# Filter layers in bfloat16 over stacked parts, and old rows of x fetched early, in a graph layer on one Trainium2 core

## The chip, the cores and the metric

The kernel runs on one core of a Trainium2 chip. Its engines are named as in the profile: PE (TensorE, the matrix products; its weight loads are PEld), DVE (VectorE), ACT (ScalarE), POOL (GpSimd) and SP (SyncE, which here only issues DMAs). Each takes its instructions in order and waits for the others by semaphores. The metric is the device time of one execution in microseconds (us).

## The reference

A graph layer with continuous filters: 12,500 nodes with 128 features (`x`), 400,000 edges sorted by target `dst` (used as the gathering index), each with 20 edge features and a weight. `smu` is a smooth activation made of a linear term and one with erf.

```python
h    = relu(layernorm(x))                       # 12500 x 128
h    = h @ W_in2f.T
Wij  = smu(edge_attr_20 @ W_f1.T + b_f1) @ W_f2.T + b_f2
Wij  = Wij * edge_weight[:, None]               # 400000 x 128
x_ij = h[dst] * Wij
agg  = segment_sum(x_ij, src, 12500)
out  = x + smu(agg @ W_o1.T + b_o1) @ W_o2.T + b_o2
```

Writing `z = f @ W_f1.T + b_f1`, the kernel uses smu(z) = gelu-like(z) + LIN * z up to a factor that is put into `w_f2`: the activation has a bent part and a linear part.

## The kernel before

Edges are cut into 3125 tiles of 128, four tiles make a group (512 edges, 782 groups), two groups a supertile (1024 edges, 391 supertiles). The supertiles are divided into nine stages ("epochs") of 59, 59, 59, 59, 48, 37, 27, 27 and 16 supertiles. Nodes are cut into 98 blocks of 128 (`NB`).

In stage k each group's messages are computed and scattered, row by row, into the DRAM buffer `buf{k}`, where each of the 98 blocks of source nodes has a fixed number of slots. While stage k runs, the buffer of stage k-1 is read back (`rw`) and summed into `agg` with products against selection matrices `se` (L690, L703, L716). After the last group comes a tail, in which the buffer of the last stage is summed and the output layers run.

The order of PE, DVE, ACT and SP is written out by hand; POOL's follows from the program. One pass of the main loop, for group g, holds steps of several groups:

- SP: `load(s + 3)` on every second group: the 20 feature rows of a supertile into one of four `fbufs` (L438), the targets broadcast over 128 partitions, `rbc` (L448), and two windows of `h`, `hw` (L462). Besides, SP clears the next stage's buffer (L178) and fetches `rw` of the stage before (L679), each waiting for the PE product that frees its buffer.
- `hide(g + 2)`: PE product of `w_f1` (row 20 of it is the bias, against a row of ones; the rows behind are zero) with the features, float32, 512 columns, into `pu` (L562). `bend(g + 2)`: ACT's gelu from `pu` to `ge` (L570). `smooth(g + 2)`: DVE adds LIN * `pu` to `ge`, giving `sm` (L578).
- `count`, `bins`, `read`, `number`: slots of the scattered rows, on DVE (L496, L540, L549) and PE (L510 to L513).
- `pick`: DVE one-hot of the targets (L471); `gather(g + 1)`: PE picks the rows of `h` (L596); `take`: ACT copies them (L604).
- `weigh(g + 1)`: PE product of `w_f2` with `sm`, float32, 512 columns, into `pw` (L615). `mix(g + 1)`: DVE multiplies (L625).
- `turn(g)`: four PE products of the messages with `w_o1` (L635). `send(g)`: ACT scales them by the edge weight `w_sb` into one of six `ms` buffers (L642, L645), and POOL issues four indirect DMAs of 128 rows each (L648), with the slot numbers `ix`.
- `parts`: PE and DVE work for the sums of the stage before.

During the first stage, `step()` deals out a list of small preparations among the groups: the rows of `h` in three bfloat16 parts each (L204 to L227, tiles `hs`), the targets, late weights, `output_bias` at the end. `hs` tiles come from the `edge` pool, two buffers.

In the tail (from L944), `ask()` fetches a unit (four blocks) of old rows of x on ACT's queue (L243) into an `hg` or `mt` tile and has POOL add the bias (L249); four units are asked for ahead, then one after each `store()`. `between()` adds agg and its gelu on POOL (L981) into an `sm` tile, `second_half()` multiplies by `w_o2` on PE (L263), `store()` adds the old rows on DVE (L267) and sends the unit out on SP (L269).

`w_sb` (edge weights), `hi_f` and `lo_b` (numbers of the source's block and row) each have a column a tile for all 3125 tiles and are read in order of the groups.

## Time and profile before

| | us |
|---|---|
| median of 3 runs | 4114.15 |
| the runs | 4108.7, 4114.17, 4114.15 |
| the profiled execution | 4108.47 |
| its span, first to last instruction | 4106.6 |
| first scatter starts | 19.9 |
| last scatter starts | 4001.5 |

The profiler's page gives the busy time of each engine, groups of instructions by line with their mean duration, and the idle time of the engine just before them with what ended most of it. "Issue" there is time in which the engine waited for nothing that the profile shows. A timeline lists instructions with start and duration. DMA share is the busy share of the 16 DMA engines. Queue q1 carries the DMAs that SP issues, q0 those of POOL. The costliest groups besides those shown below:

```profile
L645 ACT ACTIVATE ms<-pt,w_sb 128x128 f32<-128x128 f32 x3125 | 889.0, 368 | 1122.7 <-PE pt L635 1115.4
L703 PE MATMUL pg<-se,rw 128*128 128x128 f32 x8036 | 1149.1, 280 | 2.9 <-DVE se L690 2.9
L615 PE MATMUL pw<-sm,w_f 128*128 128x512 f32 x1564 | 823.0, 609 | 10.7 <-DVE sm L578 8.8
L562 PE MATMUL pu<-f,w_f 128*128 128x512 f32 x1564 | 807.3, 598 | 0.0
L578 DVE SCALAR_TENSOR_TENSOR sm<-pu,ge 128x512 f32<-128x512 f32 x782 | 535.8, 685 | 185.6 <-ACT ge L570 179.2
L596 PE MATMUL ph<-oh,hw 126*128 126x512 bf16 x770 | 297.0, 386 | 0.0
...
q1 hardware_dynamic: 449760, 601.83, 54.7%
q0 software_dynamic: 100320, 207.40, 15.9%
```

A float32 product appears as two matmul records; the busy time is that of their union.

### The profile page before, as it was taken

The page shows a single profiled execution, that of the slowest core. Times are in us where ns is not written, and L with a number is a line of the kernel's source. Part 1 is how long each engine was busy: PE and PEld are TensorE (multiplying, and loading weights), DVE is VectorE, ACT ScalarE, POOL GpSimd, SP SyncE. Part 2 cuts the span into 40 slices and gives each one's busy share as a digit, 9 for nine tenths or more (in the row PEclk, how much of TensorE's full clock was granted, in tenths as well). Part 3 has the DMA queues.
Part 4 walks back from the last instruction along what each step waited for, and adds up shares of the span by engine and source line. Part 5 has one row for each costly group of instructions (what it writes and reads, how often), then busy time and mean ns, then how long its engine had stood idle before and what let it go on. Part 6 is the DMA issues. An engine that isn't in the chain of part 4 may idle for free.

```text
span 4106.6 us, 74086 instructions
## 1 busy us (share of the span) xinstructions
PE 3668.0 (89%) x21117; PEld 2553.0 (62%) x21117; DVE 3445.1 (84%) x7657; ACT 1948.2 (47%) x5690; POOL 3081.7 (75%) x3199
## 2 busy tenths in 40 slices
PE   7878887998979998979998979999899989999897
PEld 4445545666656666646666656666677667666677
DVE  8898887888868888868888868888899889988896
ACT  4557764544444444434544434444444444444441
POOL 6777777777777777777777777777777777777775
PEclk9999999999999999999999989999999999999999
DMA  6976656776647676757667747777689699887568
GB/s 188 232 189 179 195 166 198 204 201 197 195 130 220 204 204 186 201 152 206 202 197 198 198 147 204 208 204 212 179 229 223 186 244 242 221 228 217 164 194 250
DMA packets 564246, 820.83 MB, mean 200 GB/s; under 512 B 178033, under 2 KB 378488, under 8 KB 563698
## 3 DMA queue, kind: packets, MB, share of 16 engines
q1 hardware_dynamic: 449760, 601.83, 54.7%
q0 software_dynamic: 100320, 207.40, 15.9%
q10 hardware_dynamic: 13746, 6.80, 0.6%
q8 instruction: 167, 2.74, 0.3%
q14 instruction: 253, 2.07, 0.2%
HBM read 442.34 MB, written 373.37 MB: 199 GB/s over the span
## 4 chain that ended last, share of the span: by engine, by line
PE 38%; DVE 28%; DMA 19%; ACT 6%; issue 5%; POOL 2%; DVEq 0%; SPq 0%; ACTq 0%; POOLq 0%
DMA buf<-ms,ix 17%; PE pt L635 11%; PE pg L703 8%; DVE se L690 8%; PE pw L615 8%; PE pu L562 7%; DVE mt L625 5%; DVE so L496 4%; DVE sm L578 3%; DVE sl L540 3%; ACT ms L645 2%; ACT ge L570 2%; POOL buf L648 2%; PE ph L596 2%; DVE agg L716 1%
## 5 line engine op out<-in xcount | busy, mean ns | idle before, releaser
L648 POOL DMA_INDIRECT buf<-ms,ix x3125 | 3011.3, 964 | 981.5 <-issue 384.1
L645 ACT ACTIVATE ms<-pt,w_sb 128x128 f32<-128x128 f32 x3125 | 889.0, 368 | 1122.7 <-PE pt L635 1115.4
L635 PE MATMUL pt<-w_o,mt 128*128 128x128 f32 x6250 | 883.7, 285 | 386.0 <-DVE mt L625 382.4
L703 PEld LDWEIGHTS pg<-se,rw 128*128 128x128 f32 x8036 | 1052.5, 192 | 246.5 <-issue 209.7
L703 PE MATMUL pg<-se,rw 128*128 128x128 f32 x8036 | 1149.1, 280 | 2.9 <-DVE se L690 2.9
L635 PEld LDWEIGHTS pt<-w_o,mt 128*128 128x128 f32 x6250 | 768.5, 194 | 472.9 <-DVE mt L625 468.9
L496 DVE SCALAR_TENSOR_TENSOR so<-irow_ps,hi_f,so 128x98 f16<-128x98 f32 x3116 | 989.5, 318 | 82.6
L615 PE MATMUL pw<-sm,w_f 128*128 128x512 f32 x1564 | 823.0, 609 | 10.7 <-DVE sm L578 8.8
L562 PE MATMUL pu<-f,w_f 128*128 128x512 f32 x1564 | 807.3, 598 | 0.0
L625 DVE SCALAR_TENSOR_TENSOR mt<-pw,b,hg 128x512 f32<-128x512 f32 x782 | 583.9, 747 | 201.3 <-ACT hg L604 198.0
L570 ACT ACTIVATE ge<-pu 128x512 f32<-128x512 f32 x782 | 468.4, 599 | 533.2 <-PE pu L562 524.6
L578 DVE SCALAR_TENSOR_TENSOR sm<-pu,ge 128x512 f32<-128x512 f32 x782 | 535.8, 685 | 185.6 <-ACT ge L570 179.2
L690 DVE TENSOR_TENSOR se<-irow_ps,rw 128x1536 f32<-128x1536 f32 (+1 forms) x345 | 588.0, 1704 | 114.0 <-DMA rw<-buf 109.1
L604 ACT ACTIVATE hg<-ph 128x512 f32<-128x512 f32 x782 | 468.5, 599 | 59.7 <-PE ph L596 42.9
L540 DVE TENSOR_REDUCE sl<-pc 128x4 f32<-128x392 f32 x782 | 434.7, 556 | 0.0
L642 ACT ACTIVATE ms<-lo_b 128x4 f32<-128x4 bf16 x782 | 160.1, 205 | 339.8 <-DMA buf<-ms,ix 339.4
L596 PE MATMUL ph<-oh,hw 126*128 126x512 bf16 x770 | 297.0, 386 | 0.0
L562 PEld LDWEIGHTS pu<-f,w_f 128*128 128x128 f32 x1564 | 251.9, 195 | 52.2 <-issue 40.9
L510 PE MATMUL pc<-so,tri 128*128 128x392 f16 x782 | 257.8, 330 | 0.4 <-DVE so L496 0.2
L615 PEld LDWEIGHTS pw<-sm,w_f 128*128 128x128 f32 x1564 | 241.3, 195 | 23.6 <-DVE sm L578 20.2
L512 PEld LDWEIGHTS <-rest_h 128*128 128x128 f16 x781 | 76.3, 98 | 263.1 <-issue 263.1
L512 PE MATMUL pc<-so,rest_h 128*128 128x294 f16 x781 | 225.5, 289 | 0.0
(153 smaller groups left out, 1386.9 us busy)
## 6 DMA issues: line engine op xcount, KB each, us to landing
rw<-buf SPq DMA_DIRECT2D x292, 774.0 KB
rbc<-rel_dram SPq DMA_DIRECT2D x389, 256.0 KB
buf<-zero SPq DMA_DIRECT2D x243, 387.0 KB
buf<-ms,ix POOLq DMA_INDIRECT x3125
buf<-zero SPq DMA_DIRECT2D x193, 258.0 KB
rw<-buf SPq DMA_DIRECT2D x49, 645.0 KB
f<-in_f_t SPq DMA_DIRECT2D x390, 80.0 KB
hw<-h_dram SPq DMA_DIRECT2D x770, 31.5 KB
```

The lines of the kernel that those rows point to most:

```text
L496: nc.vector.scalar_tensor_tensor(so[:, j], irow_ps[:, :NB], hi_f[:, t + j:t + j + 1], so[:, j - 1] if j else before, op0=ALU.is_equal, op1 ...
L540: nc.vector.tensor_reduce(sl[:, :n], pc[:, :n], op=ALU.max, axis=AX.X)
L562: nc.tensor.matmul(pu[:, :n], w_f1, loaded[g // PER][0][:, o:o + n], start=True, stop=True)
L570: nc.scalar.activation(ge[:, :n], units_of[g][:, :n], AF.Gelu, scale=ZS)
L578: nc.vector.scalar_tensor_tensor(sm[:, :n], units_of.pop(g)[:, :n], LIN, hidden[g][:, :n], op0=ALU.mult, op1=ALU.add)
L615: nc.tensor.matmul(pw[:, :n], w_f2, hidden.pop(g)[:, :n], start=True, stop=True)
L625: nc.vector.scalar_tensor_tensor(mt[:, :n], pws.pop(g)[:, :n], b2, rows_of.pop(g)[:, :n], op0=ALU.add, op1=ALU.mult)
L635: nc.tensor.matmul(pt[:, j, :], mt[:, j * P:(j + 1) * P], w_o1, start=True, stop=True)
L645: nc.scalar.activation(ms[:, j, 0:P], pt[:, j], AF.Copy, scale=w_sb[:, t + j:t + j + 1])
L648: i = nc.gpsimd.indirect_dma_start(out=bufs[k][:, :], out_offset=bass.IndirectOffsetOnAxis(ap=ix[:, j:j + 1], axis=0), in_=ms[:, j, :], in ...
L690: nc.vector.tensor_tensor(se[:, :m], irow_ps.unsqueeze(1).to_broadcast([P, m, P]), rows_in[c][:, :m, P:P + 1].to_broadcast([P, m, P]), op= ...
L703: nc.tensor.matmul(pgs[0][:, g, :], rows_in[c][:, o, 0:P], sel[c][:, o, :], start=(q == 0), stop=(q == Q[k] - 1))
```

## The change

From supertile 60 on (`PLAIN`; the 61st) the two filter products use bfloat16 parts. Each float32 number is written as a sum of three bfloat16 parts, and of the nine products of parts the six largest are kept. Twenty features times six products are 120 rows, and three more rows hold the parts of the bias against ones: 123 of 128 rows, one bfloat16 pass. `ws_f` holds the stacked weights of `w_f1`. `ws_c` holds those of LIN * `w_f1` * `w_f2`, the linear term of smu carried through the second layer; it is accumulated in `pw` ahead of `w_f2` times the gelu. So `smooth` does nothing for these groups.

The features come in chunks of six supertiles (`SEG`): one DMA brings 120 rows to `fx`, ACT and DVE cut them into three parts (`split`, in two halves of 512 columns each: eight steps over eight groups, two of each kind), and three DMAs a supertile copy the parts inside SBUF into the stacked rows, 60, 40 and 20 of them. Three `fbufs` of float32 remain and serve as six bfloat16 stacks; their last 32 rows are filled with bfloat16 ones. `rbc` has three buffers in place of four, `hs` tiles grow.

Six steps at the end of the list of preparations make the weights. In the last stage, one unit of old rows a group, twelve in all, is fetched on SP's queue into columns of `w_sb`, `hi_f` and `lo_b` that have been read for the last time; in the tail `ask()` fetches only the others. The tail's `sm` moves to the `msg` pool.

```diff
-    b1w = const.tile([P, P], F32, name="b1w")
...
-    lo_b = const.tile([P, NT], BF, name="lo_b")
+    lo_w = const.tile([P, NT + NT % 2], BF, name="lo_b")
+    lo_b = lo_w[:, 0:NT]
...
+    ws_f = const.tile([P, P], BF, name="ws_f")
+    ws_c = const.tile([P, P], BF, name="ws_c")
...
-        NF = 4
+        NF = 3
+        HALVES = 2
+        SEG = P // R
+        PLAIN = eps_of[0][1] + 1
         fbufs = [ld.tile([P, SUP * P], F32, name=f"f{i}", bufs=1) for i in range(NF)]
+        fx = ld.tile([P, SUP * P], F32, name="fx", bufs=1)
         def fill(i, engine):
             engine.memset(fbufs[i], 1.0)
+            engine.memset(fbufs[i][96:P, :].bitcast(BF), 1.0)
+        def stack_of(s):
+            half = s // NF % HALVES
+            return fbufs[s % NF].bitcast(BF)[:, half * SUP * P:(half + 1) * SUP * P]
...
-        fill(3, nc.gpsimd)
...
-            if s > 0:
+            if s >= PLAIN:
+                fb = stack_of(s)
+                c, j = (s - PLAIN) // SEG, (s - PLAIN) % SEG
+                a = 0
+                for q in range(3):
+                    r = 3 - q
+                    nc.sync.dma_start(fb[a:a + r * R, :n],
+                                      parts_of[c][j * R:(j + 1) * R, q, :n].unsqueeze(1).to_broadcast([R, r, n]))
+                    a += r * R
+            elif s > 0:
                 nc.sync.dma_start(fb[0:R, :n], f_t[:, e0:e0 + n])
...
+        def split(c, i):
...
+                    nc.sync.dma_start(fx[0:whole * R, :],
+                                      f_t[:, e0:e0 + whole * SUP * P].rearrange("k (s e) -> s k e", e=SUP * P))
...
+            f32, of = fx[:rows, o:o + w], lambda q: part[:rows, q, o:o + w]
+            if kind == 0:
+                nc.scalar.activation(of(0), f32, AF.Copy)
+            elif kind == 1:
+                nc.vector.tensor_sub(f32, f32, of(0))
+            elif kind == 2:
+                nc.scalar.activation(of(1), f32, AF.Copy)
+            else:
+                nc.vector.tensor_sub(of(2), f32, of(1))
+        def splits(g):
+            c, i = divmod(g - PER * (PLAIN - 3 - SEG) - 4, PER * SEG)
+            if c >= 0 and i < 8:
+                split(c, i)
+            if c >= -1 and i == 8:
+                split(c + 1, -1)
...
-            rb = ld.tile([P, SUP * P], BF, name="rbc")
+            rb = ld.tile([P, SUP * P], BF, name="rbc", bufs=3)
...
-            nc.tensor.matmul(pu[:, :n], w_f1, loaded[g // PER][0][:, o:o + n], start=True, stop=True)
+            w = w_f1 if g // PER < PLAIN else ws_f
+            nc.tensor.matmul(pu[:, :n], w, loaded[g // PER][0][:, o:o + n], start=True, stop=True)
...
-            sm = edge.tile([P, GRP * P], F32, name="sm")
-            nc.vector.scalar_tensor_tensor(sm[:, :n], units_of.pop(g)[:, :n], LIN, hidden[g][:, :n],
-                                           op0=ALU.mult, op1=ALU.add)
-            hidden[g] = sm
+            pu, ge = units_of.pop(g), hidden[g]
+            if g // PER < PLAIN:
+                nc.vector.scalar_tensor_tensor(ge[:, :n], pu[:, :n], LIN, ge[:, :n], op0=ALU.mult, op1=ALU.add)
...
-            nc.tensor.matmul(pw[:, :n], w_f2, hidden.pop(g)[:, :n], start=True, stop=True)
+            folded = g // PER >= PLAIN
+            if folded:
+                nc.tensor.matmul(pw[:, :n], ws_c, loaded[g // PER][0][:, o:o + n], start=True, stop=False)
+            nc.tensor.matmul(pw[:, :n], w_f2, hidden.pop(g)[:, :n], start=not folded, stop=True)
...
+        def homes():
+            spent = eps_of[-1][0] * SUP // (GRP * P) * (GRP * P)
+            for t in (w_sb, hi_f):
+                for o in range(0, spent, GRP * P):
+                    yield t[:, o:o + GRP * P]
+            for o in range(0, spent // 2 // (GRP * P) * (GRP * P), GRP * P):
+                yield lo_w.bitcast(F32)[:, o:o + GRP * P]
+        held = {unit: home.rearrange("p (b d) -> p b d", b=GRP)
+                for unit, home in zip([u for u in units if u[1] == GRP][::2], homes())}
+        ahead = list(held)
...
+        def crossed():
+            nc.gpsimd.memset(ws_f, 0.0)
+            nc.gpsimd.memset(ws_c, 0.0)
...
+        def stacked():
+            for w, to in zip((ws_f, ws_c), pieces()):
+                a = 0
+                for q in range(3):
+                    r = 3 - q
+                    nc.sync.dma_start(w[a:a + r * R, :], to[0:R, 0:r, :])
+                    a += r * R
+                for q in range(3):
+                    nc.sync.dma_start(w[a + q:a + q + 1, :], to[R:R + 1, q, :])
...
+        weight_steps = [crossed, combined, lambda: cut_weights(w_f1, pieces()[0]), lambda: cut_weights(lift, pieces()[1]),
+                        stacked, restored]
...
+        steps += weight_steps
...
+            if k and k == EPOCHS - 1 and i >= WAIT and ahead:
+                unit = ahead.pop(0)
+                old_rows(unit, held[unit], nc.sync)
...
             smooth(g + 2)
+            splits(g)
...
-                xr = edge.tile([P, GRP * P], F32, name=name).rearrange("p (b d) -> p b d", b=GRP)
-                old_rows(unit, xr, nc.scalar)
+                if unit in held:
+                    xr = held[unit]
+                else:
+                    xr = edge.tile([P, GRP * P], F32, name=name).rearrange("p (b d) -> p b d", b=GRP)
+                    old_rows(unit, xr, nc.scalar)
...
-            sm = edge.tile([P, GRP * P], F32, name="sm")
+            sm = msg.tile([P, GRP, ROW], F32, name="ms").rearrange("p b r -> p (b r)")[:, :GRP * P]
```

More of the change, by code (lines that the diff above doesn't have):

```diff
@@ L284, in gnn_kernel @@
         nc.vector.tensor_copy(irow_ps, irow)
-        NF = 4
+        NF = 3
+        HALVES = 2
+        SEG = P // R
+        assert SEG >= 6 and 6 * R + 3 <= P
+        PLAIN = eps_of[0][1] + 1
         fbufs = [ld.tile([P, SUP * P], F32, name=f"f{i}", bufs=1) for i in range(NF)]
+        fx = ld.tile([P, SUP * P], F32, name="fx", bufs=1)
         def fill(i, engine):
             engine.memset(fbufs[i], 1.0)
+            engine.memset(fbufs[i][96:P, :].bitcast(BF), 1.0)
+        def stack_of(s):
+            half = s // NF % HALVES
+            return fbufs[s % NF].bitcast(BF)[:, half * SUP * P:(half + 1) * SUP * P]
         FEW = 6 * SUP
         def parts_tile():
-            return edge.tile([P, GRP, 3, D], BF, name="hs")
+            whole = edge.tile([P, 3, SUP * P], BF, name="hs").rearrange("p q e -> p (q e)")
+            return whole[:, :GRP * 3 * D].rearrange("p (n k d) -> p n k d", k=3, d=D)
         early = (eps_of[0][1] + 3) * PER
@@ L441, in load, with chunk_of @@
                 targets(s)
+        parts_of = {}
+        def chunk_of(c):
+            s0 = PLAIN + c * SEG
+            return s0, min(SEG, NS - s0)
+        def split(c, i):
+            s0, m = chunk_of(c)
+            if m <= 0:
+                return
+            e0, whole = sups[s0][0] * P, sum(sups[s0 + j][1] == SUP for j in range(m))
+            rows = m * R
+            cols = sups[s0][1] * P if m == 1 else SUP * P
+            if i < 0:
+                if whole:
+                    nc.sync.dma_start(fx[0:whole * R, :],
+                                      f_t[:, e0:e0 + whole * SUP * P].rearrange("k (s e) -> s k e", e=SUP * P))
+                for j in range(whole, m):
+                    n = sups[s0 + j][1] * P
+                    e = sups[s0 + j][0] * P
+                    nc.sync.dma_start(fx[j * R:(j + 1) * R, :n], f_t[:, e:e + n])
+                return
+            if i == 0:
+                parts_of[c] = edge.tile([P, 3, SUP * P], BF, name="hs")
+            part = parts_of[c]
+            kind, half = i // 2, i % 2
+            o = half * (SUP * P // 2)
+            w = min(cols, o + SUP * P // 2) - o
+            if w <= 0:
+                return
+            f32, of = fx[:rows, o:o + w], lambda q: part[:rows, q, o:o + w]
[13 more added lines that the diff above has]
+                split(c + 1, -1)
         def targets(s):
@@ L995, in store @@
             ask()
+        while ahead:
+            unit = ahead.pop(0)
+            old_rows(unit, held[unit], nc.sync)
         for _ in range(4):
```

23 lines of the change are left out of this document (21 added, 2 removed).

## The prediction

> **What bounds the kernel now.** I read the page's busy line first, then the groups of instructions, and then looked whether the busiest engine is also the one that sets the pace.
>
> ```profile
> PE 3668.0 (89%) x21117; PEld 2553.0 (62%) x21117; DVE 3445.1 (84%) x7657; ACT 1948.2 (47%) x5690; POOL 3081.7 (75%) x3199
> ...
> L648 POOL DMA_INDIRECT buf<-ms,ix x3125 | 3011.3, 964 | 981.5 <-issue 384.1
> ```
>
> PE looks like the bound and POOL looks a quarter idle. The timeline of POOL alone, in the middle of the run, says otherwise (start, duration, then in brackets the idle time before it and what ended it):
>
> ```profile
> 1500.67 0.96 POOL L648 DMA_INDIRECT buf<-ms,ix  x1 [0.30 <-issue]
> 1501.94 0.96 POOL L648 DMA_INDIRECT buf<-ms,ix  x1 [0.30 <-ACT ms L645]
> 1503.20 0.96 POOL L648 DMA_INDIRECT buf<-ms,ix  x1 [0.30 <-issue]
> ```
>
> A scatter starts every 1.263 us whoever "released" it; the 0.30 us before each belongs to its cost. The same row counted by stage (stretch, its length, POOL busy with the count of scatters, clock, DMA share, GB/s):
>
> ```profile
> 1228.00:1826.00 598.00, 453.97 (x472) 0.98 0.66 191
> ...
> 3285.90:3561.60 275.70, 207.14 (x216) 0.98 0.91 234
> 3837.00:4002.50 165.50, 119.97 (x125) 0.97 0.68 196
> ```
>
> 598.00/472 = 1.267, 275.70/216 = 1.276, 165.50/125 = 1.324 us a scatter. So the span is: 19.9 us to the first scatter, 3124 x 1.263 = 3945.6 us of scatters back to back, 37 us in which they ran above that pace, and 105.1 us from the last one (4001.5) to the end (4106.6). Adding up every scatter one by one, 18 us of the 37 are long scatters (over 0.96 us) and 19 us are longer gaps: 7.7 in the first stage, 2.8 in the seventh, 7.6 in the last, under 1 in each other. Only the head, the 37 and the tail can be won; a step that slows a scatter is paid in full.
>
> **What slows a scatter.** Two DVE subtractions of the same size, from the groups with shapes kept apart:
>
> ```profile
> L226 DVE TENSOR_TENSOR hs<-rw,hs 128x512 bf16<-128x512 f32 x23 | 15.5, 683 | 0.0
> L222 DVE TENSOR_TENSOR rw<-pg,hs 128x512 f32<-128x512 f32 x23 | 15.5, 683 | 1.9 <-ACT hs L221 1.9
> ```
>
> L226 has both inputs in SBUF, L222 one in PSUM. On the timeline of the first stage:
>
> ```profile
> 405.00 0.68 DVE L226 TENSOR_TENSOR hs<-rw,hs 128x512 bf16<-128x512 f32 x1
> 405.16 1.36 POOL L648 DMA_INDIRECT buf<-ms,ix  x1 [0.31 <-DVE mt L625]
> ...
> 408.03 0.69 DVE L226 TENSOR_TENSOR hs<-rw,hs 128x512 bf16<-128x512 f32 x1
> 408.08 1.47 POOL L648 DMA_INDIRECT buf<-ms,ix  x1 [0.30 <-DVE sl L540]
> ```
>
> The scatter that begins while L226 runs takes 1.36 and 1.47 us instead of 0.96. The extra is the time from its start to L226's end, less 0.12: 405.69 - 405.16 - 0.12 = 0.41 (seen 0.40), 408.72 - 408.08 - 0.12 = 0.52 (seen 0.51). The other seven overlaps of over 0.05 us obey it to 0.01 us; an L226 that starts after the scatter's start costs nothing. L471 (bf16 to bf16 in SBUF) obeys it too, 12.9 us in 390 operations. The DVE rows with one operand in PSUM (L496, L578, L625, L690, L716) leave the median at 0.958.
>
> **The change, part by part.**
>
> **Filter passes (groups 120 to 781, 662 groups).** PE loses one f32 128x512 matmul a group (L562: 807.3/782 = 1.03 us) and gains two bf16 ones of 512 columns (as L596: 0.386 each at most; a quarter of the f32 product's 0.86 in the chain of waits, 0.215, at least): 0.26 to 0.60 us less a group, about 0.4. DVE loses L578: 0.685 us a group. ACT's L570 stays. In a stage bound by POOL this is worth only the longer gaps that PE and DVE cause: 2.8 + 7.6 in the seventh and last stages. I take -8 us (0 to -10).
>
> **Splits.** 331 supertiles in chunks of six make 55 full chunks and one of five tiles. Each chunk costs four ACT copies (L225: 0.64 us) and four subtractions of 120x512. ACT: 220 x 0.64 = 141 us on an engine 47% busy, hidden by the idle time of L645 (1122.7 us); uncovered it would be 0.2 us a group. DVE: 220 x 0.683 = 150 us, less than the 453 us of L578. But all 220 read two SBUF operands (fx and the part), as L226 does. By the rule above an operation of 0.683 us delays the next scatter if it starts 0.56 to 0.03 us ahead of it, by 0 to 0.53 us: averaged over a period of 1.263 us that is 0.53²/2/1.263 = 0.111 us; L226 itself averaged 2.75/25 = 0.110. Where L578 starts now, relative to the scatters, a 0.683 us operation would give 0.128. 220 x 0.111 to 0.128 = 24 to 28 us: I take **+25 us** (0 to +35; no row excludes that the f32 output of the first kind differs).
>
> The Trainium skill speaks against this sum. "SBUF — State Buffer", section "Who interferes with whom", says that a two-input tensor operation takes only the read side of the port shared with GpSimd, and infers that descriptor generation, which writes, is not held up. By that the term would be 0. The trace disagrees, with 0.40 and 0.51 us beside L226; the same section's other rule, that two SBUF inputs contend with a GpSimd operation that reads SBUF, fits a scatter that reads its indices, and by that the sum stays.
>
> **Loads.** The 80 KB f load a supertile becomes a sixth of a 480 KB fx load (same bytes) and three copies inside SBUF, 60+40+20 rows of 2 KB = 240 KB. 331 x 240 KB = 79 MB, 10% on 820.8. At q1's mean (54.7% of 16 x 4106.6 us for 601.83 MB: 60 ns a KB) that is 14 us of queue time, 0.9 us of all 16 queues in the 10.1 us of a supertile: +0.09 DMA share. Hidden where the share is 0.66 to 0.71; in the seventh stage it is 0.91 (0.97 to 0.99 over some 100 us), where rw could come late. +3 us (0 to +12). SP issues two more DMAs a supertile (0.4 us each, of 10.1). The new wait, SP on the last split once a chunk, holds back rbc, hw, the clears and the rw fetches behind it; the split was issued a group earlier and rbc is used two groups (10 us) later, so nothing, or a group's 5 us each time if DVE were that late. Three f and rbc buffers in place of four: the reader that frees them ran a group earlier; nothing, at worst +2.
>
> **Weights (once, end of first stage).** Two POOL memsets in the scatter queue (as L392: 0.19 us, and 0.3 around each), ten small DVE and ACT operations, two PE passes, twelve DMAs on SP: +1 us, hidden but for POOL.
>
> **Fills.** The start of the trace:
>
> ```profile
> 3.89 5.10 DVE L304 CAST ssf<-ss 128x48 f32<-128x48 int32 x1
> ...
> 7.62 0.44 POOL L407 MEMSET zr<- 128x384 bf16 x1
> 7.97 0.97 POOL L290 MEMSET f<- 128x1024 f32 x1
> ```
>
> A 48-column cast stands 5.10 us until POOL's row of memsets is over, and all DVE work for the first scatter is behind it. The change takes one 0.97 us memset out and puts in two of 2048 bf16 columns. L407 gives 0.44 us for 384, L290 0.97 for 1024 f32: 0.9 us if bytes count, 1.9 if elements do. That is +0.8 to +2.8 us, and up to +1.5 more if the longer DVE fill pushes L754 into the same block. I take +3 (0 to +4.5).
>
> **Tail.** Stretches of the tail (PE, PEld, DVE, ACT, POOL, clock, DMA share, GB/s) and pieces of the chain of waits:
>
> ```profile
> 4000.00:4050.00 50.00, 42.02 (x335) 40.55 (x333) 36.35 (x40) 7.88 (x12) 26.96 (x25) 0.93 0.92 280
> 4050.00:4090.00 40.00, 33.73 (x283) 32.21 (x284) 27.31 (x31) 7.94 (x11) 30.07 (x25) 1.00 0.90 272
> ...
> 4034.48 5.77 DMA hg<-in_x
> 4040.42 1.24 POOL hg L249
> 4041.66 1.24 POOL sm L981
> ```
>
> The tail alternates between waiting for old rows of x and 0.9 DMA share. It moves 12.9 MB of rw, 6.4 of x and 6.4 of out, 25.7 MB in 93 us. Twelve of the 256 KB loads (3.1 MB) move from ACT's queue to SP's in the last stage, where the share is 0.68 (+18 GB/s on 196: hidden; 11 us if it were not). 22.6 MB at the same rate take 82 us: -11. By the chain every second 5.8 us wait falls away, until PE (84% busy) binds: 93 x 0.16 = -15 at most. I take **-10 us** (-4 to -15). The sums' new place in the msg pool leaves ys three units (10 us) of buffers against an output DMA of some 5: nothing.
>
> **Sum.** +3 + 25 + 1 + 3 - 8 - 10 = +14, on the profiled execution's 4108.47 us: 4122.5. That execution is at the low end of the runs (4108.7, 4114.17, 4114.15; median 4114.15), so I add about half the distance: **4125 us**.
>
> **Rivals.**
> *The scatters aren't held up* (the page's inference, or the splits fall behind the scatters' starts): without the 25 us, 4100 us. For it: that sentence, and L226 is only 26 operations; against it: nine overlaps to 0.01 us. 0.10.
> *PE is the bound*: 662 x 0.4 = 265 us gone, 3846 us. For it: 89%; against it: a scatter each 1.263 us in all stages. 0.03.
> *Not slower by the tail and the gaps*: the lock costs 22, weights and loads 4, the tail gives its 15, the gaps 10 and the head 0: 4108.5 + 1, with the half distance 4112 us. It decides where the tail leaves the DMA rate for PE's. 0.13.
> *DMA binds in the sixth and seventh stages*: share 0.97 + 0.09 over 150 us and late rw fetches, 12 us in place of 3, with 30 us of lock: 4139 us. For it: 0.91 share; against it: 2.8 us of gaps there now. 0.12.
> *The forecast*: 0.62, own range 4113 to 4138.
>
> **Numbers.** The range 4106 to 4143 takes in the third and fourth and leaves out the first two. 0.2% is 8 us, about what a measurement of this kernel can tell from no change. Slower: most of the forecast and all of the fourth, 0.63; within: the rest of the forecast and most of the third, 0.23; faster: the first two and a rest, 0.14.
>
> **What would show it.** Mean scatter over 0.97 us in the stages after the first, with long ones wherever a split overlaps a start (right) or 0.96 beside splits (wrong); gaps of the last stages gone; first scatter at some 23 us; last DMA wait of the tail in every second unit only and 95 us after the last scatter. Wrong above all if the scatters' pace isn't what the new total follows.

## The result, and the profile after

The changed kernel takes 4160.34 us (median of 4 runs, 4157.75 to 4165.54), the kernel before 4113.42 us beside it: 1.0119 times as long, 95% interval 1.0105 to 1.0132. That is 46.9 us more, where 11 were forecast, and above the range. The profiled execution took 4165.54 us, with a span of 4163.7 us. It is the longest of its four, and the profiled execution of the kernel before (4108.47 us) is as short as the shortest of its own, so the profiles lie 57 us apart where the medians lie 47.

Busy line and costliest group of the page after:

```profile
PE 3467.2 (83%) x20793; PEld 2588.9 (62%) x21120; DVE 3173.2 (76%) x7226; ACT 2088.2 (50%) x5919; POOL 3113.1 (75%) x3202
...
L722 POOL DMA_INDIRECT buf<-ms,ix x3125 | 3039.0, 972 | 997.7 <-issue 365.1
```

PE has 201 us less to do and DVE 272, and the span is 57 us longer. What grew is the row of the scatters: 972 ns in the mean, not 964, and 16 us more idle time ahead of them (work that stands between two scatters isn't in that figure). So the pace of the scatters is still what the total follows. The scatters by stage (stretch, its length, POOL busy with the count of scatters, clock, DMA share, GB/s), the third, seventh and last:

```profile
1239.20:1842.00 602.80, 458.88 (x473) 0.95 0.74 214
3316.40:3603.40 287.00, 210.61 (x217) 0.94 0.88 245
3886.60:4065.30 178.70, 121.06 (x125) 0.96 0.74 217
```

The third stage is 4.8 us longer, with long scatters; the seventh 11.3 and the last 13.2 us longer, with nearly the same busy time: there it is gaps. Adding up every scatter as for the prediction (excess of each over 0.958 us, of each gap over 0.305 us):

| us | before | after | difference |
|---|---|---|---|
| to the first scatter | 19.9 | 22.9 | +3.0 |
| long scatters | 20.1 | 47.9 | +27.8 |
| longer gaps, first stage | 7.7 | 11.9 | +4.2 |
| second to sixth | 1.1 | 2.5 | +1.4 |
| seventh and eighth | 2.8 | 17.1 | +14.3 |
| last | 7.6 | 19.6 | +12.0 |
| last scatter to the end | 105.1 | 99.6 | -5.5 |
| **span** | 4106.6 | 4163.7 | +57.1 |

(The rows add up to 57.2 by rounding.) The same sums are made for each experiment below. They are worked out from one profiled execution each, and identical code scatters in them: four executions that don't differ up to the eighth stage (the changed kernel twice, and two in which only the bias additions are moved) had gaps of 17.1, 28.1, 29.5 and 31.0 us in the seventh and eighth. The first of them, in the table, is the low one. Long scatters vary too: 42.8 to 47.9 us in these four; 20.1 in the kernel before and 25.5 in an experiment that adds nothing ahead of its last stage.

**Long scatters.** Timeline of DVE, then of POOL, in the third stage of the kernel after:

```profile
1309.94 0.68 DVE L499 TENSOR_TENSOR fx<-fx,hs 120x512 f32<-120x512 f32 x1
...
1327.16 0.68 DVE L503 TENSOR_TENSOR hs<-fx,hs 120x512 bf16<-120x512 f32 x1
```
```profile
1310.23 1.23 POOL L722 DMA_INDIRECT buf<-ms,ix  x1 [0.31 <-ACT ms L716]
...
1327.24 1.44 POOL L722 DMA_INDIRECT buf<-ms,ix  x1 [0.30 <-DVE mt L699]
```

By the rule of the prediction the extra is 1309.94 + 0.68 - 1310.23 - 0.12 = 0.27 us (seen 0.27) and 1327.16 + 0.68 - 1327.24 - 0.12 = 0.48 (seen 0.48). Over the whole run 150 scatters begin while a split subtraction runs, and they are 29.5 us longer than 0.958 us each: 15.5 us beside L499 (f32 output), 14.0 beside L503 (bf16 output). The rule gives 31.9 us, with a median misfit of 0.007 us a scatter.

**Gaps late in the run.** A chain in the eighth stage. The queue of SP's DMAs (start, duration of the issue):

```profile
3831.87 0.86 SPq L480 DMA_DIRECT2D fx<-in_f_t  x1
3832.83 0.41 SPq L753 DMA_DIRECT2D rw<-buf  x1
3833.29 0.50 SPq L180 DMA_DIRECT2D buf<-zero  x1
3833.83 2.73 SPq L455 DMA_DIRECT2D f<-hs  x3
3836.60 1.10 SPq L518 DMA_DIRECT2D rbc<-rel_dram  x1
```

The 480 KB of features go out, then a fetch of 774 KB, the three copies of stacked parts, and only then `rbc`, from which `oh` of a coming group is made. On DVE's and then POOL's timeline:

```profile
3847.81 0.49 DVE L541 TENSOR_SCALAR oh<-rbc,prow 128x1024 bf16<-128x1024 bf16 x1 [4.89 <-DMA rbc<-rel_dram]
```
```profile
3852.07 0.96 POOL L722 DMA_INDIRECT buf<-ms,ix  x1 [0.31 <-issue]
3855.87 0.96 POOL L722 DMA_INDIRECT buf<-ms,ix  x1 [2.84 <-ACT ms L719]
```

DVE stands 4.89 us for `rbc`, until 11 us after its issue, and 8 us later the scatter stands 2.84 us in place of 0.30: 2.5 us lost. "ACT ms" is the last link, not the cause. Waits of DVE over the whole run (waiting line, what it waited for, total us, times, the longest), before and then after:

```profile
DVE se L690 <- DMA rw<-buf: 109.1, 9, 20.8
```
```profile
DVE se L764 <- DMA rw<-buf: 159.4, 23, 21.1
...
DVE oh L541 <- DMA rbc<-rel_dram: 50.7, 26, 4.9
```

The second wait is new: before there was none on `rbc`. Some 39 of the 50.7 us fall on the supertile whose `rbc` is issued right behind an `fx` load.

`rbc` isn't alone. The waits for `rw` rose from 9 to 23; most of their total is one long wait near the start of each stage, which the kernel before has too, and the shorter ones are new. One of these, on DVE and then on POOL, in the seventh stage:

```profile
3493.39 1.76 DVE L764 TENSOR_TENSOR se<-irow_ps,rw 128x1536 f32<-128x1536 f32 x1 [3.74 <-DMA rw<-buf]
```
```profile
3498.62 0.96 POOL L722 DMA_INDIRECT buf<-ms,ix  x1 [3.71 <-ACT ms L719]
```

As far as the profile tells what released each step, a gap can be followed back to the first transfer that was waited for. In this profile seven gaps of the seventh and eighth stage exceed the usual one by more than 0.8 us, 15 us together: 8.1 lead to `rbc`, 5.8 to `rw` and 1.1 to an earlier scatter's own write, on which the next use of an `ms` buffer waits. In the second profile of the same kernel (below) there are eleven, 24.8 us: 11.3 lead to `rw`, 10.4 to scatters' own writes and 3.1 to `rbc`. So several transfers come late there, and which one ends a gap changes from execution to execution.

`rbc` also has less time than it had. From the end of its issue to the start of its one-hot the median was 17.0 and 19.3 us in the seventh and eighth stage before, and is 9.5 and 8.6 us now. SP has more to issue (DMAs, then duration in ns, lowest/median/highest), before and then after:

```profile
L438 SPq DMA_DIRECT2D f<-in_f_t x390: 287/394/3687, 5.8 to 3962.2; - x195
```
```profile
L455 SPq DMA_DIRECT2D f<-hs x993: 742/827/4638, 597.2 to 4019.8; - x199
```

Three copies at 0.83 us in place of one load at 0.39 are 2.1 us more a supertile, where the prediction had two more DMAs of 0.4 us. Whether this shortens the time of `rbc`, or its third buffer in place of the fourth, no run separates.

**Gaps of the last stage.** POOL's timeline there:

```profile
3927.32 0.96 POOL L722 DMA_INDIRECT buf<-ms,ix  x1 [0.30 <-issue]
3928.30 1.29 POOL L251 TENSOR_TENSOR w_sb<-w_sb,bo 128x512 f32<-128x512 f32 x1
3929.75 0.97 POOL L722 DMA_INDIRECT buf<-ms,ix  x1 [0.17 <-issue]
```

L251 adds the bias to a unit of old rows. Before, all of it stood in the tail; now the twelve units fetched early have it between two scatters: 1.47 us from one to the next in place of 0.30. Eight such gaps (1.17 over), two with a pair of additions (2.38 over) and one wait of 5.79 us make 9.3 + 4.8 + 5.5 = 19.6, the whole excess of the stage. The wait of 5.79 us follows one of DVE for `rw`, 11.19 us long.

### The profile page after: what moved, and what is told of

The parts are those of the page before. It is cut to its first block, busy times and chain, and to the rows that moved or that the text cites. A ratio compares the mean times of both kernels' runs of the same rounds, so it can differ in the third digit from the quotient of the medians.

```text
span 4163.7 us, 74923 instructions
## 1 busy us (share of the span) xinstructions
PE 3467.2 (83%) x20793; PEld 2588.9 (62%) x21120; DVE 3173.2 (76%) x7226; ACT 2088.2 (50%) x5919; POOL 3113.1 (75%) x3202
## 5 line engine op out<-in xcount | busy, mean ns | idle before, releaser
L709 PE MATMUL pt<-w_o,mt 128*128 128x128 f32 x6250 | 917.8, 292 | 590.0 <-DVE mt L699 586.9
L777 PEld LDWEIGHTS pg<-se,rw 128*128 128x128 f32 x8036 | 1065.5, 194 | 264.8 <-issue 226.9
L709 PEld LDWEIGHTS pt<-w_o,mt 128*128 128x128 f32 x6250 | 791.9, 199 | 687.8 <-DVE mt L699 682.6
L689 PE MATMUL pw<-ge,w_f 128*128 128x512 f32 x1564 | 853.4, 629 | 33.0 <-DVE ge L650 11.8
L689 PEld LDWEIGHTS pw<-ge,w_f 128*128 128x128 f32 x1564 | 303.7, 200 | 57.9 <-DVE ge L650 24.4
L580 PE MATMUL pc<-so,tri 128*128 128x392 f16 x782 | 258.9, 331 | 27.0 <-DVE sl L610 25.5
L633 PE MATMUL pu<-f,ws_f 128*128 128x512 bf16 x659 | 253.0, 384 | 0.0
L541 DVE TENSOR_SCALAR oh<-rbc,prow 128x1024 bf16<-128x1024 bf16 x385 | 190.5, 495 | 50.8 <-DMA rbc<-rel_dram 50.7
L666 PEld LDWEIGHTS <-hw 126*128 126x128 bf16 x770 | 78.2, 102 | 200.0 <-issue 166.6
L790 DVE TENSOR_TENSOR agg<-agg,pg 128x512 f32<-128x512 f32 (+1 forms) x200 | 134.2, 671 | 68.0 <-PE pg L777 67.8
```

The source lines that it names most:

```text
L666: nc.tensor.matmul(ph[:, :n], hw[:3 * WIN, g % PER, :], oh[:3 * WIN, o:o + n], start=True, stop=True)
L689: nc.tensor.matmul(pw[:, :n], w_f2, hidden.pop(g)[:, :n], start=not folded, stop=True)
L709: nc.tensor.matmul(pt[:, j, :], mt[:, j * P:(j + 1) * P], w_o1, start=True, stop=True)
L777: nc.tensor.matmul(pgs[0][:, g, :], rows_in[c][:, o, 0:P], sel[c][:, o, :], start=(q == 0), stop=(q == Q[k] - 1))
```

## The experiments

### The first chip

Four kernels went to a chip on which the kernel before took 5092.81 us, 24% more. *No early rows*: no unit is fetched in the last stage. *Bias in the tail*: the additions wait for a copy of the bias made in the tail. *PSUM operand*: the split subtractions take their first operand from a PSUM tile of index numbers. *Light copies*: from the second round on, the three copies move an eighth of the columns.

```diff
# no early rows
-                for unit, home in zip([u for u in units if u[1] == GRP][::2], homes())}
+                for unit, home in zip([], homes())}
# bias in the tail
+        nc.vector.tensor_copy(lift, bo2)
...
-                with_bias(unit, xr, nc.gpsimd)
+                with_bias(unit, xr, nc.gpsimd, lift if unit in held else None)
# PSUM operand
-                nc.vector.tensor_sub(f32, f32, of(0))
+                nc.vector.tensor_sub(f32, irow_all[:rows, :w], of(0))
...
-                nc.vector.tensor_sub(of(2), f32, of(1))
+                nc.vector.tensor_sub(of(2), irow_all[:rows, :w], of(1))
# light copies
-                    nc.sync.dma_start(fb[a:a + r * R, :n],
+                    m = n if s < PLAIN + 2 * NF else n // 8
+                    nc.sync.dma_start(fb[a:a + r * R, :m],
```

> The changed kernel, but no old rows of x are fetched in the last stage; all are fetched in the tail as before. Theory: the 12 bias additions of 1.28 us that POOL runs between the last stage's scatters cost some 14 us and the shorter tail gives 5.5 back. Then the last stage's longer gaps fall from 19.6 to about 6 us, the tail goes from 99.6 back to about 105 us, and the time from 4160 to about 4152 us. Rival: the last stage is late because of the DMA load alone and the additions fill idle time; then the gaps stay near 19 us and the time rises to about 4165 us.

> The changed kernel, early loads kept, but the bias of the early rows is read from a copy that DVE makes only after the first selection of the tail, so that POOL's twelve additions come behind the last scatter. Theory (the additions cost the scatters 1.17 us each): the last stage's longer gaps fall by 13 to 14 us, the tail grows by 0 to 12 us since the additions now stand ahead of the sums, time 4146 to 4159 us. Rival (the 12 loads, not the additions): gaps stay at 19 us, time 4160 to 4172 us.

> The changed kernel with the first operand of the 220 split subtractions read from a PSUM bank (constants) in place of fx in SBUF: same count, shape and length of DVE work, values of the parts left wrong. Theory (two SBUF inputs hold up a scatter that begins meanwhile): the excess of long scatters falls from 47.9 to 18 to 22 us, about what the kernel before shows (20.1), and the time by 24 to 30 us to about 4133 us. Rival (scatters are long because the DMA queues carry more): excess stays near 48 us and the time near 4160 us.

> The changed kernel with the three stack copies a supertile cut to an eighth of their columns from the 67th supertile on: same DMAs issued on SP, same waits, 30 KB in place of 240 KB; the rest of the stacked rows is left as it was. Theory (the DMA engines are full in the sixth to ninth stage and rw comes late): longer gaps of stages five to nine fall from 39 to about 14 us (the bias additions), time about 4137 us. Rival (the copies' issue and waits on SP hold up the rw fetches): gaps and time stay as they are, 4155 to 4162 us.

Ratios 1.0248 [1.0183, 1.0313], 1.0220 [1.0176, 1.0264], 1.0218 [1.0171, 1.0265] and 1.0178 [1.0134, 1.0221]. The scatters' row of the first of them:

```profile
L722 POOL DMA_INDIRECT buf<-ms,ix x3125 | 3030.7, 970 | 2066.6 <-ACT ms L719 1237.7
```

A scatter takes what it took, but POOL stands idle 1069 us longer than in the kernel after above, in gaps in every stage, at a granted clock of 0.887. Where something else sets the pace, the terms of a pace set by scatters can't be read from the time, and the changed kernel itself has no run on that chip: inconclusive. What can be used is the excess of long scatters, 40.3, 38.1, **25.1** and 38.0 us: only the PSUM operand lowers it. And the tail without early rows, 105.9 us, against 91.2 to 100.1 in the three with them. Three of the four were run again elsewhere.

### One part at a time

On chips where the kernel before takes 4111 to 4113 us. *Early rows alone* is the kernel before with the twelve units fetched in the last stage on SP's queue, their bias added in the tail, and no stacks or splits.

> The kernel before with one part of the change alone: twelve units of old rows fetched in the last stage, their bias additions placed behind the last scatter by a copy of the bias that DVE makes in the tail. No stacks, no splits. Theory (the tail waits for old rows and for DMA rate): scatters as before, tail from 105 to 91 to 100 us, time 5 to 14 us under the kernel before (4100 to 4109 us where that takes 4113). Rival (the additions stand ahead of the sums on POOL and eat the gain): within 3 us of the kernel before.

> e3 once more, since its chip ran the kernel before in 5093 us and left POOL waiting in every stage. On a chip at the pace of the first profiles: theory (two SBUF inputs hold up scatters): excess of long scatters 18 to 22 us in place of 47.9, time 24 to 30 us under the changed kernel, some 4133 us, ratio to the kernel before 1.004 to 1.006 in place of 1.012. Rival (DMA load lengthens the scatters): excess near 48 us, ratio 1.012.

> e4 once more on a chip at the pace of the first profiles. Theory (full DMA engines make rw late in stages six to nine): longer gaps of stages five to nine 39 to about 14 us, time some 4137 us, ratio 1.005 to 1.007. Rival (issue and waits on SP): gaps and ratio (1.012) stay.

> e2 once more on a chip at the pace of the first profiles. Theory (the bias additions between the scatters cost 1.17 us each): longer gaps of the last stage 19.6 to 5 to 7 us, tail 93 to 105 us in place of 99.6, time 4142 to 4155 us, ratio 1.007 to 1.010. Rival (they fill idle time): gaps 19 us, ratio 1.012 or more.

| | ratio, 95% | long | gaps: first stage | 7th + 8th | last | tail |
|---|---|---|---|---|---|---|
| changed | 1.0119 [1.0105, 1.0132] | 47.9 | 11.9 | 17.1 | 19.6 | 99.6 |
| early rows alone | 0.9981 [0.9972, 0.9991] | 25.5 | 8.6 | 2.6 | 6.9 | 99.2 |
| PSUM operand | 1.0071 [1.0053, 1.0089] | 18.8 | 9.3 | 29.9 | 19.2 | 95.8 |
| light copies | 1.0062 [1.0045, 1.0078] | 50.4 | 10.1 | 4.6 | 17.2 | 92.0 |
| bias in the tail | 1.0113 [1.0096, 1.0130] | 42.8 | 11.2 | 29.5 | 9.7 | 99.6 |

The early rows pay by themselves, 7 us. The PSUM operand takes 29 us of long scatters away and 20 us of time (0.0048 x 4113), less than the 24 to 30 expected; the subtractions are still there, of the same duration, but the 128 scatters that begin beside them are only 0.4 us longer in all. The third stage of that kernel, in the columns used above:

```profile
1233.20:1831.20 598.00, 453.42 (x472) 0.96 0.75 216
```

598.0 in place of 602.8 us, as long as before the change. The light copies take 23 us, within what was expected; SP issues as many DMAs as in the changed kernel, and the gaps of the seventh and eighth stages are 4.6 us, against 17.1 to 31.0 in the executions of the changed code there. The bias additions in the tail take 10 us from the last stage (13 to 15 were expected), and yet only 2 to 3 us from the total.

### The additions once more, everything at once, and a PSUM operand for the one-hot

The changed kernel again, unmodified, beside *bias in the tail*; the three edits (PSUM operand, light copies, bias in the tail) together; and a step of its own: the rule of the prediction also covers the one-hot comparison (`oh`, 390 operations, 12.9 us of long scatters), so in *one-hot from PSUM* the early rows alone get it in a form with a PSUM operand, a column of ones, in the first five stages.

```diff
-            nc.vector.tensor_scalar(oh[:, :n], loaded[s][1][:, :n], pcol if s < FEW // SUP else prow, None, op0=ALU.is_equal)
+            col = pcol if s < FEW // SUP else prow
+            if s < eps_of[5][0]:
+                nc.vector.scalar_tensor_tensor(oh[:, :n], loaded[s][1][:, :n], col, irow_ps[:, 1:2].to_broadcast([P, n]),
+                                               op0=ALU.is_equal, op1=ALU.mult)
```

> The changed kernel itself, as the yardstick of this set: 4157 to 4166 us where the kernel before takes 4112, ratio 1.0105 to 1.0132. Longer gaps of the seventh and eighth stage together anywhere from 15 to 30 us, as e7, whose code is the same up to there, showed 29.5 and the first profile 17.2.

> The twelve bias additions moved behind the last scatter, as in e7, against e9 on the same chip and with more rounds, since e7's gaps fell by 10 us in the last stage and its time by 1. Theory (each addition between two scatters is paid): 8 to 12 us under e9. Rival (the last stage is held by DMA at its start anyway, and what the scatters win there is waited for elsewhere): within 4 us of e9.

> Three parts at once on the changed kernel: subtractions with a PSUM operand (values left wrong), stack copies cut to an eighth from the 67th supertile on (the rest left as it was), bias additions in the tail. Theory (lock, DMA load and additions are the whole loss): long scatters 18 to 20 us, longer gaps 18 to 28, tail 90 to 95, time 4098 to 4110 us, under the kernel before. Rival (a cost not named yet, on SP or ACT, remains): 4118 us or more.

> e8 (early rows alone on the kernel before, additions in the tail) with the one-hot of the targets in the first five stages computed with a second operand from PSUM, so that it runs without the port that scatters need; correct values, DVE's operation longer (some 1.1 in place of 0.48 us, 242 times). Theory (the lock costs each scatter that begins during L471): excess of long scatters from 25.5 to 8 to 14 us, time 8 to 14 us under e8 (4091 to 4097). Rival (the longer operation delays messages more than it frees scatters, or the scatters aren't freed): within 4 us of e8's 4105 or above.

| | median, us | ratio, 95% | long | gaps: first stage | 7th + 8th | last | tail |
|---|---|---|---|---|---|---|---|
| changed again | 4163.21 | 1.0124 [1.0108, 1.0139] | 44.7 | 11.1 | 28.1 | 17.8 | 94.6 |
| bias in the tail | 4160.98 | 1.0115 [1.0100, 1.0131] | 44.7 | 11.0 | 31.0 | 8.0 | 100.0 |
| all three | 4111.16 | 0.9998 [0.9989, 1.0007] | 21.9 | 10.1 | 9.2 | 8.4 | 96.0 |
| one-hot from PSUM | 4124.63 | 1.0037 [1.0023, 1.0050] | 11.1 | 29.8 | 2.2 | 7.0 | 100.5 |

The additions: 10 us less in the last stage, 5 more in the tail, 2 in the total, within the intervals; 8 to 12 were expected. That the tail takes back part of what the stage gives isn't shown: the two profiles of the changed kernel differ by 5 us in the tail themselves. The three edits together bring the kernel back to the time of before and no further, where 4098 to 4110 us was expected: some cost is left.

The one-hot does free the scatters: 0.2 us of long ones in each of the second to fourth stages, with 594.6 to 595.8 us from first to last scatter against 596.9 to 598.5 for the early rows alone. But the new form takes 1.27 us where the old takes 0.48, and in the first stage DVE, already busy 503 of 608 us, is then busy 531: gaps of 29.8 us. What was expected of the total failed.

### The one-hot where there is room, and no splits

*One-hot in three stages* keeps that form to the second to fourth stages (`eps_of[1][0] <= s < eps_of[4][0]`). *No splits* is *all three* without any `fx` load, copy to parts or subtraction after the first chunk, whose parts all later stacks use.

```diff
         def split(c, i):
+            if c > 0:
+                if i >= 0:
+                    parts_of[c] = parts_of[0]
+                return
```

> e12 with the PSUM form of the one-hot in the second to fourth stage alone, where e12 left 0.2 us of long scatters and under 1.5 us of gaps a stage, and the old form elsewhere, where the longer operation cost gaps (29.8 us in the first stage). Theory (a scatter is held up by DVE's use of the port, and where DVE has room the long form is free): 7 to 10 us under e8, 4094 to 4098 us where the kernel before takes 4111, ratio 0.996 to 0.9975. Rival (the saved scatter time is waited for in later stages or the tail): as e8, ratio 0.998 or above.

> e11 with the split done for the first chunk alone: no fx loads, no ACT copies and no DVE subtractions after it, all later stacks taken from the first chunk's parts. e11 came out level with the kernel before, where 4098 to 4110 was expected. Theory (what is left in e11 is the split's own work, on ACT and DVE and in the fx loads of the seventh stage): gaps of the stages after the first fall from 20 to about 10 us and the time to 4096 to 4103 us. Rival (it is the start, the first stage and the order of the last stages' work, which PE's and DVE's relief doesn't touch): 4106 to 4112 us, gaps as in e11.

| | median, us | ratio, 95% | long | gaps: first stage | 7th + 8th | last | tail |
|---|---|---|---|---|---|---|---|
| one-hot in three stages | 4098.19 | 0.9965 [0.9953, 0.9978] | 18.8 | 9.9 | 4.8 | 5.6 | 103.8 |
| no splits | 4096.65 | 0.9965 [0.9952, 0.9977] | 18.8 | 10.2 | 3.0 | 1.3 | 95.9 |

By its median the first is faster than both kernels: 13.5 us under the 4111.72 us of the kernel before beside it, and 6.8 us under the early rows alone, measured in another set, where the intervals of the two ratios just overlap. Its profile comes from its longest execution, 4108.03 us, level with the profile of the early rows alone: 6.7 us less of long scatters, 2.6 more of gaps, 4.6 more of tail. So the freed scatters are seen there, but not the gain in time. Its third stage, in the columns used above:

```profile
1230.40:1827.00 596.60, 452.57 (x472) 0.98 0.66 192
```

596.60/472 = 1.264 us a scatter, against 1.267 before: nothing left to win there but the pace itself.

The second shows what remained in *all three*: some 14 us go with the splits and their `fx` loads. Its granted clock was 0.957, as in the other kernels with stacks (0.951 to 0.960, against 0.976 to 0.980 without), and it is 15 us faster than the kernel before: the lower clock isn't what the changed kernel lost by. The last stage there:

```profile
3840.80:4000.00 159.20, 119.83 (x125) 0.95 0.77 221
```

159.2 us against 165.5 before: this is what the lighter filter layers are worth when nothing is charged for them.

### The load of the features

Which part of the splits is it? In the changed kernel, *fx in pieces* issues the 480 KB of a chunk as six loads of 80 KB, two at each of three groups (`split` then loads the rows of two supertiles a call); *no fx loads* loads only the first chunk. Copies, subtractions and additions stay in both.

```diff
# fx in pieces: in splits(g)
-            if c >= -1 and i == 8:
+            if c == -1 and i == 8:
                 split(c + 1, -1)
+            elif c >= 0 and 8 <= i < 11:
+                split(c + 1, 6 - i)
# no fx loads
-            if c >= -1 and i == 8:
+            if c == -1 and i == 8:
                 split(c + 1, -1)
```

> The changed kernel with each 480 KB fx load replaced by six of 80 KB, two in each of three groups; correct values. In the changed kernel DVE waits 51 to 57 us for rbc (nothing in the kernel before), 38 of the 51 for the second supertile of a chunk, whose rbc load is issued right behind fx. Theory (the burst of fx stands ahead of rbc in the queue): these waits fall under 20 us, gaps of the seventh and eighth stage from 17 to 28 to about 10 us, time 8 to 15 us under the changed kernel's 4160 to 4163. Rival (SP comes late to the loads because it waits for the splits): waits and time as in the changed kernel.

> The changed kernel without the fx loads after the first chunk; the splits go on cutting what stands in fx, at the same instructions and waits, so later filters are wrong. Theory (the fx burst delays rbc and with it the messages): DVE's waits for rbc under 10 us, gaps of the seventh and eighth stage under 10 us, time 12 to 20 us under the changed kernel. Rival (the copies alone fill the queues, or SP's wait for the splits does it): waits for rbc above 30 us and time within 6 us of the changed kernel.

| | median, us | ratio, 95% | long | gaps: first stage | 7th + 8th | last | tail |
|---|---|---|---|---|---|---|---|
| fx in pieces | 4151.96 | 1.0098 [1.0083, 1.0114] | 41.1 | 7.2 | 21.2 | 14.2 | 101.2 |
| no fx loads | 4130.99 | 1.0048 [1.0034, 1.0062] | 42.6 | 7.3 | 0.1 | 14.3 | 93.9 |

Without the loads 29 to 31 us go (ratio differences 0.0071 and 0.0076 to the two measurements of the changed kernel); in pieces 9 to 11. More went without them than the 12 to 20 expected. They are also bytes that the kernel before moved, so the 29 to 31 us are not the price of the change. The waits of DVE without the loads:

```profile
DVE se L764 <- DMA rw<-buf: 159.8, 14, 21.0
...
DVE oh L541 <- DMA rbc<-rel_dram: 7.3, 9, 1.5
```

The wait for `rbc` went, from 50.7 to 7.3 us, and the seventh and eighth stages have no excess of gaps. `rw` is waited for as long in total, but 14 times in place of 23, so its short waits became fewer too. From issue to one-hot `rbc` has 9.3 and 7.4 us in these two stages, no more than in the changed kernel: the short time costs only together with the load. The rival by which SP waits for the splits finds no support: at the `fx` loads of the changed kernel SP's only listed wait is 2.9 us, for `rw`.

In pieces, the wait for `rbc` fell nearly as forecast, and yet the gaps of these stages stayed at 21.2 us where about 10 were expected. Two lines of that kernel's waits:

```profile
DVE oh L540 <- DMA rbc<-rel_dram: 20.3, 14, 3.3
...
ACT hs L494 <- DMA fx<-in_f_t: 66.8, 18, 9.2
```

The second is a wait of its own making: the last pieces are issued two groups before ACT cuts the chunk, and 8.3 of the 21.2 us lead back to that wait. So `rbc` isn't the whole of the loss, and this run doesn't price the burst alone. And the seventh stage without the loads, against 287.00 us above:

```profile
3304.80:3581.10 276.30, 210.44 (x217) 0.97 0.88 250
```

The DMA share is 0.88 in both kernels: the mean share tells nothing here.

## Why the prediction was wrong in size and right in direction

**What bounds.** Right. (The prediction's parts of the span add up to 1 us more than 4106.6, within the rounding of the pace.) The rival by which PE binds (3846 us) fell: 201 us of PE went and the kernel became slower.

**The lock.** Right: +25 forecast, +27.8 in the first profile, 24.6 in the second; 0.13 us a subtraction against 0.111 to 0.128. The open question of the f32 output is answered: L499 costs as much as L503. The rival that scatters aren't held up (4100 us) fell: with one input in PSUM, the same subtractions cost 0.4 us in all. What the Trainium skill infers in "SBUF — State Buffer", section "Who interferes with whom", that such an operation doesn't hold up descriptor generation, doesn't carry over to these scatters, which took 29.5 us longer. The section's rule on two SBUF inputs and a GpSimd operation that reads SBUF agrees with both runs. Whether it is the reading of the indices that waits, no run tells.

**The fills.** Right: +3 forecast, +3.0 in the first profile and +0.9 to +3.0 over the runs of the changed kernel. The two memsets on POOL's timeline:

```profile
6.32 1.80 POOL L298 MEMSET f<- 32x2048 bf16 x1
...
10.06 1.80 POOL L298 MEMSET f<- 32x2048 bf16 x1
```

1.8 us each, at the end of the bounds at which elements count, not bytes.

**The loads: the step that failed.** The whole term was put at +3 (0 to +12): the `fx` load at nothing ("same bytes"), the copies hidden by a share that left room, two more issues on SP at 0.4 us, one buffer less at "nothing, at worst +2". The runs showed it several times larger: lightening the copies took 23 us, cutting the `fx` load in pieces 9 to 11, leaving it out 29 to 31. These don't add, since either of the first and the last clears most of the gaps of the seventh and eighth stages. The working had asked for the mean DMA share and for a late `rw`. A late `rw` is part of it (5.8 us of gaps in the first profile, 11.3 in the second). It had not asked what stands right behind 480 KB in the same queue, which is `rbc`, nor what becomes of the scatters' own writes. It took the 10 us from the issue of `rbc` to its use for enough; that is about what `rbc` has now (9.5 and 8.6 us), but before the change it had 17 to 19 us in these stages. "Nothing, or a group's 5 us each time" was written for a wait on the split; the delay came from transfers instead, up to 4.9 us at a time for `rbc` in the first profile and 6.6 in the second.

How the loss divides between the burst, the bytes of the copies and the shorter time of `rbc` is not settled. A spread of the load over all twelve groups of a chunk, with `rbc` issued ahead of it, and a fourth `rbc` buffer weren't tried.

**The relief of PE and DVE.** -8 was forecast in the gaps of the seventh and last stages. It is there only when nothing is charged for it: with no splits the last stage's gaps are 1.3 us against 7.6, while the first stage's are 10.2 against 7.7 and those of the seventh and eighth together 3.0 against 2.8. In the changed kernel it was buried: the gaps grew by 32 us in the first profile.

**The bias additions: not seen.** The prediction moved the fetches of the twelve units and priced their DMAs, but not the additions that follow them on POOL, though POOL's order sets the pace. They are 14.1 us of the last stage's 19.6. In the total they weigh 2 to 3 us by the medians, within the intervals. Where the rest of the 14 us goes stays open: with the additions moved there, the tail was 5 us longer in one pair of profiles and equal in the other.

**The tail.** -10 was forecast (-4 to -15); -5.5 in the first profile, -10.5 in the second. The price was right within the scatter; the early rows alone took 5.9 us from the tail and 7 from the time, without the rest.

**The sum.** Forecast: head +3, lock +25, memsets of the weights +1, loads +3, gaps -8, tail -10: +14. First profile: +3, +28, gaps of all kinds +32, tail -5.5: +57. Of the 43 us between them 36 are gaps (+32 against -8 + 3 + 1). The rival "DMA binds in the sixth and seventh stages" (4139 us) had the right resource and, in late `rw` fetches of the seventh stage, part of the mechanism; its place (the mean share) and its price (12 us) were wrong: the sixth stage gained 1.1 us of gaps, the seventh and eighth 14.3.

The first stage's +4.2 us of gaps in the first profile (9 to 12 us in the other runs with stacks, 7.2 and 7.3 in the two with other or no loads of `fx`) has no experiment of its own and stays open; without stacks and with the first stage as it was before, the kernels had 7.7 to 9.9.

## What to carry to other kernels

Bytes that stay the same aren't free for that: where the queues are nearly full, list every transfer that can come late, what is issued right behind a burst in the same queue above all, and measure how long before its use each is issued, before the change and after it. The mean share doesn't tell. When a fetch is moved, price what its consumer does and on which engine, above all on the one that sets the pace. And where scatters issued by GpSimd set it, give overlapping DVE operations an operand in PSUM, but only where DVE has the time that the other form takes.

## What the runs showed of the hardware

- A scatter is also held up by the one-hot comparison, bf16 with one tensor input in SBUF at 0.48 us for 1024 columns; with a PSUM operand beside it the same work takes 1.27 us, and the long scatters of a stage, 2.4 to 3.7 us in the early rows alone, fall to 0.2 us in one kernel and 0.7 to 1.0 in the other.
- A memset of 2048 bf16 columns on 32 partitions took 1.80 us on POOL, one of 1024 f32 columns on 128 partitions, as many bytes a partition, 0.97, and one of 384 bf16 columns on 128 partitions 0.44: the columns count, not the bytes.
- Issuing one copy of stacked parts inside SBUF took SP 0.83 us (median of 993), one load of 20 feature rows 0.39 (median of 390).
- On the chips where the kernel before takes 4111 to 4113 us, the profiled executions of all kernels with bf16 stacks were granted a clock of 0.951 to 0.960, those without 0.976 to 0.980.
- On one chip the kernel before took 5093 us in place of 4112, at a granted clock of 0.917 in its median run, and the changed ones had 1030 to 1070 us more of idle time ahead of scatters, in all stages. What sets the pace there wasn't sought.
